# Late loads of a self-product kernel, laid out over 13, 14 and 15 of the 16 DMA engines

## The chip, the cores and the metric

The kernel runs on one core of a Trainium2 chip. The metric is the time of one execution on the device in microseconds (us). The core has five instruction engines (of which this kernel keeps VectorE, GpSimd and SyncE busy; ScalarE helps at the start, TensorE only passes a semaphore on) and 16 DMA engines that carry all transfers between the chip's main memory and its on-chip buffer of 128 partitions.

## The reference

```
dot = jnp.einsum('bi,bj->bij', inputs, inputs)      # inputs: (4096, 256) float32
iu, ju = jnp.triu_indices(256)
return dot[:, iu, ju]                               # (4096, 32896) float32
```

Each of 4096 rows of 256 numbers becomes the 32896 products x[i]*x[j] with i <= j. The input has 4.2 MB, the output 539 MB.

## The kernel before

A partition holds 32 rows of the input. They are worked through in 8 passes (h = 0 to 7) of 4 rows; a pass has two halves of two rows, and each half is cut into three pieces along the 32896 columns. So a pass has six pieces (p = 0 to 5), and there are 48 in all. A piece is computed into one of two places in the on-chip buffer (`places`, 128 partitions x 2 rows x about 10,960 floats) by VectorE (L281) and GpSimd (L382), which multiply runs of the row by one of its numbers, and it is then stored by one transfer that SyncE issues (L410). A store has two packets for each partition, 256 of about 44 KB, so 16 on each of the 16 DMA engines. A place may be filled again only when all packets of its store have landed (the semaphores `free`), so at any time one store is under way and the next is queued behind it.

The input for passes 0, 1 and 2 is loaded by SyncE at the start (L441). The rest comes late, from GpSimd, between its products (`late`, L340 to L361): the unit `ONE` is passes 3 and 4, `EVEN` is pass 5, `TWO` is passes 6 and 7. For a row (a partition) of `ONE` or `TWO` two stretches of 1024 floats are fetched, so two packets of 4 KB; for a row of `EVEN` one packet.

The table `LATE` (L21) says when and how: each line has the pass and piece at whose begin GpSimd issues, the unit, and a list of pairs. The first part of a pair lists the sizes of small loads (`mark`, L325: that many partitions, 64 floats each, into a buffer that nobody reads), the second is the number of partitions that the load proper covers (L354). A load whose count of partitions is 20 is spread over 10 engines with two partitions each, 45 over 15 with three, 3 over three with one, 60 over 15 with four, 128 over all 16 with eight. A load begins on the engine behind the last one of the load before it, all counted around the 16. The marks have only this use: they move the engine on which the next load begins. The table `HAD` (L28) says before which piece GpSimd waits until the loads of a unit, and the marks, have landed (L358 to L361).

Counted through from engine 0, the five lines of the table before give each engine this many 4 KB packets:

| engine | before |
|---|---|
| 4 | 8 |
| 0, 1, 2, 3, 15 | 36 each |
| 5, 9 to 14 | 44 each |
| 6, 7, 8 | 48 each |

Together 640, which is 128 partitions x 5 passes.

Of the kernel before, what the change touches and what calls it, by code (L numbers as in the profile page):

```python
# [18 lines left out]
GAP = 32  # L19
ONE, EVEN, TWO = (3, 4), (5,), (6, 7)  # L20
LATE = [  # L21
    ((1, 3), ONE, [((5,), 20), ((6,), 45)]),
    ((2, 3), ONE, [((2,), 3), ((12,), 60)]),
    ((3, 3), EVEN, [((), 128)]),
    ((4, 3), TWO, [((8, 9), 20), ((6,), 45)]),
    ((5, 3), TWO, [((2,), 3), ((12,), 60)]),
]
HAD = [((2, 5), ONE, 4, 0), ((4, 5), EVEN, 1, 0), ((5, 5), TWO, 4, 9)]  # L28
HELPED = 1
HELP = 16.5  # L30
MARK = 32
# [111 lines left out]
def kernel(  # L143
# [185 lines left out]
    def inputs(of_passes: tuple, rows: slice, lo: int = 0, hi: int = rounds * each) -> tuple:  # L329
        first, last = of_passes[0], of_passes[-1]  # L330
        ends = []
        for ap, at, step in (
            (flat, first * (rounds * each + GAP), (last - first) * (rounds * each + GAP)),
            (x_in, ROUND[first] * rounds * each, (ROUND[last] - ROUND[first]) * rounds * each),
        ):
            dims = [[step, 2], [1, hi - lo]] if step else [[1, hi - lo]]
            ends.append(window(ap[rows, at + lo :], dims))
        return tuple(ends)

    def late(h, p: int):  # L340
        at, rows = 0, {}
        for (begun, piece), of_units, parts in LATE:
            with ExitStack() as when:
                if p == piece:
                    when.enter_context(nc.gpsimd.If(h == begun))
                for steps, count in parts:
# [6 lines left out]
                    if p == piece:  # L353
                        nc.gpsimd.dma_start(*inputs(of_units, slice(row, row + count))).then_inc(far[of_units], 16)  # L354
        for (had, piece), of_units, count, count_of_marks in HAD:
            if p == piece:
# [127 lines left out]
```

## Time and profile before

| | |
|---|---|
| time, median of 3 runs | 1261.2 us (1261.03 to 1261.32) |
| span of the profiled execution | 1259.5 us |
| VectorE busy | 822.7 us, 65% |
| GpSimd busy | 763.5 us, 61% |
| DMA engines | tenths 9 in 39 of 40 slices, 8 in the last |
| bytes | 4.21 MB read, 538.97 MB written, 431 GB/s over the span |

The profiled execution's own time outside the profiler is not listed; its span, from the first to the last instruction, is 1.7 us below the median of the runs. The views used further on are the page with its queues, the waits of the compute engines, GpSimd's timeline around the late loads, and the DMA view of short stretches. In the last one a stretch is cut into 40 slices, and the row GB/s counts a packet's bytes in the slice in which it starts: in a stretch as long as one packet each DMA engine shows up as one spike.

### The profile page before, as it was taken

The numbers are of one execution on the slowest core, as the hardware profiler recorded it, in microseconds if no ns is written. First come the engines' busy times: TensorE is split into PE (matmuls) and PEld (weight loads), VectorE is DVE, ScalarE is ACT, GpSimd is POOL, SyncE is SP. The second block draws the span as 40 slices with busy tenths as digits, with TensorE's granted clock in tenths as the row PEclk, the third lists the DMA queues.
The fourth block names the chain that finished last, engine by engine and source line by source line (L and its number), as shares of the span: only waits on it lengthen the run. The fifth ranks groups of instructions, "written<-read, shape, count | busy, mean of one in ns | idle before, by whom it ended". The sixth has DMA issues, their size and how long they took to land. (4 is left out here: it accounts for less than half of the span.)

```text
span 1259.5 us, 2827 instructions
## 1 busy us (share of the span) xinstructions
DVE 822.7 (65%) x1236; ACT 27.1 (2%) x74; POOL 763.5 (61%) x1149
## 2 busy tenths in 40 slices
DVE  8767657676576665766657675676656766567650
ACT  8000000000000000000000000000000000000000
POOL 5666647665476654766558665576645765467650
DMA  9999999999999999999999999999999999999998
GB/s 396 433 445 423 443 427 433 433 442 427 434 436 432 430 434 435 434 430 441 427 438 433 426 438 427 441 428 438 431 437 428 440 428 437 432 435 432 438 431 380
DMA packets 15911, 543.24 MB, mean 431 GB/s; under 512 B 1440, under 2 KB 1440, under 8 KB 3360
## 3 DMA queue, kind: packets, MB, share of 16 engines
q1 hardware_dynamic: 14704, 540.54, 99.3%
q0 software_dynamic: 1200, 2.64, 0.5%
q14 instruction: 7, 0.06, 0.0%
HBM read 4.21 MB, written 538.97 MB: 431 GB/s over the span
## 5 line engine op out<-in xcount | busy, mean ns | idle before, releaser
L281 DVE TENSOR_TENSOR o<-xv,xp 128x504 f32<-128x504 f32 (+59 forms) x1175 | 791.2, 746 | 398.1 <-DMA out_dram<-o 268.2
L382 POOL TENSOR_TENSOR o<-xv 128x64 f32<-128x64 f32 (+61 forms) x1125 | 751.6, 709 | 450.0 <-DVE o L281 449.8
L309 ACT ACTIVATE o<-x 128x198 f32<-128x198 f32 (+34 forms) x72 | 25.5, 448 | 0.8 <-DMA x<-in_r_inputs_dram 0.8
L260 DVE COPY xp<-x 128x512 f32 x15 | 10.3, 685 | 0.0
L242 DVE TENSOR_TENSOR o<-x,xp 128x470 f32<-128x470 f32 (+18 forms) x19 | 9.7, 585 | 0.0
L242 DVE TENSOR_TENSOR o<-x 128x510 f32<-128x510 f32 (+9 forms) x10 | 5.7, 647 | 2.5 <-DMA x<-in_r_inputs_dram 2.5
L258 DVE COPY xv<-x 128x512 f32 x15 | 6.5, 433 | 0.5
L366 POOL MEMSET xv<- 128x1 f32 x1 | 0.1, 99 | 10.3 <-POOLq L193 10.3
L327 POOL DMA_DIRECT2D marks<-in_r_inputs_dram x9 | 5.7, 637 | 0.4 <-issue 0.3
L354 POOL DMA_DIRECT2D x<-in_r_inputs_dram x9 | 5.5, 615 | 0.0
L444 ACT ACT_TABLE_LOAD x1 | 1.3, 1283 | 1.2 <-ACTq L193 1.2
L442 DVE MEMSET edge<- 128x32 f32 x1 | 0.1, 85 | 1.0 <-SPq L182 1.0
L237 DVE COPY xp<-x 128x512 f32<-128x512 f32 x1 | 0.7, 686 | 0.0
L367 POOL COPY xv<-x 128x512 f32<-128x512 f32 x1 | 0.6, 611 | 0.0
L444 ACT ACTIVATE edge<-edge 128x1 f32<-128x1 f32 x1 | 0.3, 295 | 0.0
L471 POOL MEMSET const-float32-0.0<- 128x1 f32 x1 | 0.1, 99 | 0.2 <-issue 0.2
L471 POOL MEMSET const-bfloat16-1.0<- 128x1 bf16 x1 | 0.1, 103 | 0.0
L471 POOL MEMSET const-uint8-127<- 128x1 uint8 x1 | 0.1, 103 | 0.0
L471 POOL MEMSET const-float32-1.0<- 128x1 f32 x1 | 0.1, 99 | 0.0
## 6 DMA issues: line engine op xcount, KB each, us to landing
out_dram<-o SPq DMA_DIRECT2D x31, 10944.0 KB, 35.2
out_dram<-o SPq DMA_DIRECT2D x16, 11008.0 KB, 32.8
out_dram<-o SPq DMA_DIRECT2D x1, 4352.0 KB, 13.8
out_dram<-o SPq DMA_DIRECT2D x1, 2624.0 KB, 9.4
out_dram<-o SPq DMA_DIRECT2D x1, 1984.0 KB, 7.2
out_dram<-o SPq DMA_DIRECT2D x1, 1280.0 KB, 5.2
x<-in_r_inputs_dram SPq DMA_DIRECT2D x1, 1024.0 KB, 4.9
x<-in_r_inputs_dram POOLq DMA_DIRECT2D x2, 480.0 KB, 29.2
```

The lines of the kernel that those rows point to most:

```text
L237: nc.vector.tensor_copy(xp, x_of(h, 0)).then_inc(v_own, 1)
L242: ins = nc.vector.tensor_tensor(place[:, :, at - lo : at - lo + length], window(x_of(h, 0)[:, j:], [[d, REPEAT], [1, 1], [1, length]]), wi ...
L258: ins = nc.vector.tensor_copy(xv[:, :each], x_of(h, p // PIECES))
L260: nc.vector.tensor_copy(xp, x_of(h, p // PIECES)).then_inc(v_own, 1)
L281: ins = nc.vector.tensor_tensor(place[:, :, at : at + m * length], window(xv[:, j:], [[d, REPEAT], [1, m], [1, length]]), window(xp[:, i:] ...
L309: nc.scalar.activation(places[p][:, r, at - lo : at - lo + length], xa[:, r * d + j : r * d + j + length], AF.Copy, scale=xa[:, r * d + i ...
L327: nc.gpsimd.dma_start(marks[lo:hi, :, :MARK], of).then_inc(marked, 16)
L354: nc.gpsimd.dma_start(*inputs(of_units, slice(row, row + count))).then_inc(far[of_units], 16)
L367: nc.gpsimd.tensor_copy(xv[:, :each], x_of(0, 0)).then_inc(g_own, 1)
L382: ins = nc.gpsimd.tensor_tensor(place[:, :, at : at + m * length], window(xv[:, j:], [[d, REPEAT], [1, m], [1, length]]), window(xv[:, i:] ...
L444: nc.scalar.activation(edge[:, :1], edge[:, 1:2], AF.Copy, scale=edge[:, 2:3])
L471: nc = _bacc.Bacc("TRN2", target_bir_lowering=False, num_devices=1)
```

## The change

Only the two tables are changed. The loads cover other numbers of partitions: 26 and 39 (13 engines with two and three partitions each), 42 and 14 (14 engines with three and one), 60, 75 and 120 (15 engines with four, five and eight), and 8 (eight engines with one). Where a pass loaded 3 and 60 partitions, it now loads 60 or 75 in one transfer; `EVEN`, which was one transfer of 128 partitions, becomes one of 8 and one of 120. The marks have other sizes, and `HAD` has other counts to match: three transfers for `ONE` and `TWO`, two for `EVEN`, eight marks.

```
 LATE = [
-    ((1, 3), ONE, [((5,), 20), ((6,), 45)]),
-    ((2, 3), ONE, [((2,), 3), ((12,), 60)]),
-    ((3, 3), EVEN, [((), 128)]),
-    ((4, 3), TWO, [((8, 9), 20), ((6,), 45)]),
-    ((5, 3), TWO, [((2,), 3), ((12,), 60)]),
+    ((1, 3), ONE, [((5,), 26), ((3,), 42)]),
+    ((2, 3), ONE, [((2,), 60)]),
+    ((3, 3), EVEN, [((), 8), ((9,), 120)]),
+    ((4, 3), TWO, [((8, 9), 39), ((3,), 14)]),
+    ((5, 3), TWO, [((2,), 75)]),
 ]
-HAD = [((2, 5), ONE, 4, 0), ((4, 5), EVEN, 1, 0), ((5, 5), TWO, 4, 9)]
+HAD = [((2, 5), ONE, 3, 0), ((4, 5), EVEN, 2, 0), ((5, 5), TWO, 3, 8)]
```

GpSimd's queue before piece 3 of passes 1 and 2 (each group ends with a branch; `marks` and `x` are the tiles that are loaded, the first number behind them is the count of partitions; - is before, + is after):

```order
 L327 DMA marks<-in_r_inputs_dram 5x2x32
-L354 DMA x<-in_r_inputs_dram 20x2x1024
-L327 DMA marks<-in_r_inputs_dram 6x2x32
-L354 DMA x<-in_r_inputs_dram 45x2x1024
+L354 DMA x<-in_r_inputs_dram 26x2x1024
+L327 DMA marks<-in_r_inputs_dram 3x2x32
+L354 DMA x<-in_r_inputs_dram 42x2x1024
 L343 UNCONDITIONAL_BRANCH
 L345 COMPARE_AND_BRANCH
 L327 DMA marks<-in_r_inputs_dram 2x2x32
-L354 DMA x<-in_r_inputs_dram 3x2x1024
-L327 DMA marks<-in_r_inputs_dram 12x2x32
```

Pass 1 keeps four transfers with other sizes; from pass 2 the load of 3 partitions and the mark of 12 are gone, and the load of 60 follows the mark of 2 directly.

GpSimd's queue before piece 3 of passes 3 and 4, with the same names:

```order
-L354 DMA x<-in_r_inputs_dram 128x1024
+L354 DMA x<-in_r_inputs_dram 8x1024
+L327 DMA marks<-in_r_inputs_dram 9x2x32
+L354 DMA x<-in_r_inputs_dram 120x1024
 L343 UNCONDITIONAL_BRANCH
 L345 COMPARE_AND_BRANCH
 L327 DMA marks<-in_r_inputs_dram 8x2x32
 L327 DMA marks<-in_r_inputs_dram 9x2x32
-L354 DMA x<-in_r_inputs_dram 20x2x1024
-L327 DMA marks<-in_r_inputs_dram 6x2x32
-L354 DMA x<-in_r_inputs_dram 45x2x1024
+L354 DMA x<-in_r_inputs_dram 39x2x1024
```

Pass 3 has three transfers where one stood, pass 4 as many as before with other sizes. In all GpSimd issues 16 transfers where it issued 18. No product moves on any engine.

Counted through from engine 0 in the same way, the changed table gives these counts of 4 KB packets:

| engine | before | after |
|---|---|---|
| 4 | 8 | 1 |
| 3 | 36 | 26 |
| 2 | 36 | 34 |
| 0, 1, 15 | 36 | 44 |
| 5, 9, 10, 11 | 44 | 45 |
| 6, 7, 8 | 48 | 45 |
| 12, 13, 14 | 44 | 44 |

## Rows read from the trace of the kernel before

**Rows 1.** The page: DMA in 40 slices, and the queues (packets, MB, share of 16 engines).
```profile
DMA  9999999999999999999999999999999999999998
...
q1 hardware_dynamic: 14704, 540.54, 99.3%
q0 software_dynamic: 1200, 2.64, 0.5%
```

**Rows 2.** Who waited for whom: us in total, times, longest us.
```profile
POOL o L382 <- DVE o L281: 449.8, 46, 11.1
DVE o L281 <- DMA out_dram<-o: 268.2, 31, 10.2
```

**Rows 3.** The page: stores by issue, KB each, median us from issue to landing.
```profile
out_dram<-o SPq DMA_DIRECT2D x31, 10944.0 KB, 35.2
```

**Rows 4.** Line L354, GpSimd's late loads: from issue to landing.
```profile
DMA to landing us min/median/max: 11.1/19.7/31.8
```

**Rows 5.** GpSimd's timeline, passes 2 and 3: start, us, what, [idle before <- releaser].
```profile
366.58 0.66 POOL L354 DMA_DIRECT2D x<-in_r_inputs_dram  x1
373.96 14.87 POOL L382 TENSOR_TENSOR o<-xv 128x908 f32<-128x908 f32 x12 [6.73 <-DVE o L281]
...
521.40 0.63 POOL L354 DMA_DIRECT2D x<-in_r_inputs_dram  x1
530.65 14.87 POOL L382 TENSOR_TENSOR o<-xv 128x908 f32<-128x908 f32 x12 [8.62 <-DVE o L281]
```

**Rows 6.** Late-load queue in stretches 212:240, 368:398, 525:542, 681:714, 838:867, one row each.
```profile
q0 software_dynamic: 256, 0.54, 4.9%
...
q0 software_dynamic: 256, 0.52, 4.4%
...
q0 software_dynamic: 144, 0.52, 7.5%
...
q0 software_dynamic: 288, 0.54, 4.2%
...
q0 software_dynamic: 256, 0.52, 4.6%
```

**Rows 7.** 1.623 us from 999.062, 1076.708, 1154.354, 1232.0: GB/s in 40 slices each.
```profile
GB/s 0 0 0 0 0 0 2170 1085 0 1085 1085 0 0 0 0 1085 1085 0 0 0 0 0 0 0 0 0 1085 0 0 0 0 1085 1085 0 1085 2170 0 1085 0 1085
...
GB/s 0 0 0 0 0 0 1085 1085 0 1085 1085 0 0 0 1085 1085 1085 0 0 0 0 0 0 0 0 0 1085 0 0 0 0 1085 1085 0 1085 2170 0 1085 0 2170
...
GB/s 0 0 0 0 0 0 1085 1085 0 1085 1085 0 0 0 1085 0 1085 0 0 0 0 0 0 0 0 1085 1085 0 0 0 0 1085 1085 0 1085 2170 0 1085 0 2170
...
GB/s 0 0 0 0 0 0 1085 1085 0 1085 1085 0 0 0 1085 0 1085 0 0 0 0 0 0 0 0 0 1085 0 0 0 0 1085 1085 0 1085 3256 0 1085 0 2170
```

**Rows 8.** The last packets, stretch 1254.599:1256.222: GB/s in 40 slices of 0.0406 us, packets.
```profile
GB/s 1085 0 1085 1085 0 0 0 0 0 1085 1085 0 0 1085 0 0 0 0 1085 1085 0 0 0 0 0 0 0 0 0 0 0 0 0 0 0 0 0 0 1085 0
DMA packets 16, 0.40 MB, mean 244 GB/s; under 512 B 7, under 2 KB 7, under 8 KB 7
```

## The prediction

> **What bounds the kernel now.** I read the page's queues first. The 16 DMA engines are busy in every slice, and the stores' queue alone holds 99.3% of their time [rows 1]. So nothing can be won by computing faster, and the waits say the same from the other side: VectorE stands 268 us waiting for stores to free a place, GpSimd 450 us waiting for VectorE [rows 2]. A store lands 35.2 us after its issue [rows 3], while its 10,944 KB (11.2 MB) at 431 GB/s take 26 us, so about 9 us of the store before it are still ahead of it in the queues. As long as no DMA engine falls more than about 9 us behind another, none runs dry: each of the 16 works through its own list without a gap, and the execution ends when the slowest one has done its list. The question is which one that is, and what the change does to its list.
>
> Two views answer. In stretches as long as one packet each engine is one spike. Four such stretches, each 77.646 us (three stores) behind the last, show fifteen spikes that stay in their slices and one that moves: counting slices from 0, it is the second packet in slice 6, then the one in 14 or 15, then 25, then the third packet in 35 [rows 7]. That is some 10 slices of 0.0406 us, 0.4 us, in 77.6 us: one engine loses about 0.5 us in every 100 us against all others, 6 us over the whole run. Slice 35 of the last stretch is 1233.4; fourteen packets of 1.623 us later it is 1256.15, and in the last stretch that is the start of the very last packet, in slice 38 [rows 8]. So the drifting engine is the one that ends the run. The two behind it start their last packets in slices 18 and 19 (1255.33 and 1255.37), 0.8 us sooner; then come slice 13 (1.0 us sooner), 10 and 9 (1.15), 3, 2 and 0 (1.45 to 1.55); the seven others had started theirs before the stretch, and its seven small packets are their completions, so all sixteen start their last within some 3 us.
>
> Which engine drifts? The price of a load packet is read from pass 3, where the late queue has 144 packets, of which 128 are the 0.52 MB: 7.5% of 16 engines over 17 us are 20.4 us, 0.16 us for each of the 128 [rows 6]. By the count through the table, engine 4 has 8 of them, the others 36 to 48, so it has 28 to 40 x 0.16 = 4.5 to 6.4 us less to do. An engine with that little work and no slowness would end 4 us before the rest. None does; so engine 4 is the one that loses the 6 us. That the count through the table holds is seen in the packets: if a load gives every one of the 16 engines as many packets as the fullest one has, data or a placeholder, and one more to signal, the five lines come to 256, 256, 144, 288 and 256, which are the rows to the packet, 1200 in all [rows 1, 6]. In the first, for instance, marks of 5 and 6 give 32 each, 20 partitions over 10 engines 16 x 5 = 80, 45 over 15 engines 16 x 7 = 112.
>
> Here a page of the Trainium skill states how the engines are chosen: DMA: Bandwidth & Descriptors, section "Why a DMA increments its semaphore by 16 and not by 1", says that GpSimd's loads go to consecutive engines from a round-robin cursor. By that rule the count through the table is right, and the packet counts of this trace agree with it as far as they go (they name no engine).
>
> **The change, part by part.** *The packets that move.* A load packet that takes the place of a small one costs 0.16 less the small one's time. That is about 0.01: in the first stretch 4.9% of 16 x 28 us are 21.9 us, 130 full packets' worth of bytes take 20.7, and some 126 small ones the rest [rows 6]. The new table gives 256, 176, 208, 256 and 208, in all 1104 packets, six fewer on each engine: -0.06 us for all. So:
> - engine 4: 7 load packets fewer, -1.05 - 0.06 = -1.1 us;
> - engine 3: 10 fewer, -1.6; engine 2: 2 fewer, -0.4;
> - engines 0, 1 and 15: 8 more, +1.2 - 0.06 = +1.1;
> - engines 6, 7, 8: 3 fewer, -0.5; engines 5, 9, 10, 11: 1 more, +0.1; engines 12 to 14: -0.06.
>
> All of it lies on the path if the engine is the last one, none if it is not.
>
> *GpSimd's issues.* Pass 3 has two transfers more to issue at 0.6 us each, 1.2 us; there GpSimd then stands idle for 8.6 us until VectorE releases it, so this is hidden; pass 2 (and pass 5, with the same list) has two fewer, and its 6.7 us of idle time only grow [rows 5]. Zero. Without that cover the 1.2 us would go into one piece, and the 9 us of queued store would still hide it.
>
> *When the data is there.* The loads of a line landed 11 to 32 us after the issue [rows 4]; the wait for them stands two pieces later at the soonest, 52 us at 26 us each. In pass 3 three transfers now follow each other, 208 packets where 144 stood, and each of an engine's load packets goes between two stores (7.5% of the time to loads of 0.16 us against stores of 1.6): 13 in place of 9, some 6.5 us longer, used more than a pass later. Zero. Behind the waits for fewer transfers stands GpSimd's last piece of the pass, as before.
>
> *Which engine is last afterwards.* Engine 4 falls by 1.1 and is no longer the last, unless its drift grows. The next two stand at -0.8, and who they are no row says. Of fifteen candidates three rise by 1.1 (0, 1, 15), five fall by 0.4 to 1.6 (2, 3, 6, 7, 8), seven stay. If the three are not among the two latest (12/15 x 11/14 = 0.63 by count alone), then the end moves by -0.8 if those two stay and no one rises past them, by +0.1 if one of the three stood at -1.0, by 0.0 if at -1.15, by -0.4 if at -1.5. I take -0.3, between the two ends, nearer to the engines at -1.15 and -1.5, of which there are five against one at -1.0. If one of the three is among the two latest, the end moves by -0.8 + 1.1 = +0.3.
>
> **The rivals.** *One of engines 0, 1 or 15 becomes the last (slower).* The mechanism above, decided by where that engine ends now: later than 1.1 us ahead of the last, and the run becomes longer. Price up to +0.3 to +0.4: 1261.6. For it: three of the fifteen candidates; against it: only two places are late enough to matter by more than 0.1.
>
> *Engine 15 or 7 is a slow one.* What it would do here: were engine 15 one of the two at -0.8, its 8 packets more would cost up to twice their price, as the slow one's: -0.8 + 2.4 = +1.6, 1262.8. Rows speak against it: only one spike drifts [rows 7], and it is the one with next to no loads. The Trainium skill, DMA: Bandwidth & Descriptors, "Latency and other measured facts", says that engines 7 and 15 are usually slower than the others; by that rule loads would be kept off engine 15, and this trace does not bear it out.
>
> *The loads don't land where the count says.* If the first load begins on another engine than in the run before, the drifting engine gets 44 or 45 packets in place of 8: 36 x 0.15 = +5.4, 1266.6. Against it: the five lines move the starting engine by 148 in all, both before and after, so even a start that is carried on from one execution to the next would be carried alike, and the small spread of the runs, 0.3 us, shows no such jumps.
>
> *It does nothing:* the last engine stays where it was because the drift takes what the loads give back, 1261.2.
>
> **How the numbers follow.** The span is 1259.5, the median 1261.2; I take the 1.7 us around the span as unchanged. Forecast: 1261.2 - 0.3 = 1260.9, with 0.58. One of 0, 1, 15 last, 1261.6: 0.29. No change, 1261.2: 0.06. Engine 15 slow, 1262.8: 0.04. Another start, 1266.6: 0.03. The range reaches from the lower end of the forecast with the runs' spread, 1261.2 - 0.8 - 0.3 = 1260.1, to the upper end of the first rival with it and a little of the loads' contention, 1262.0. About 0.2%, 2.5 us, is what a measurement of this kernel can tell from no change. Only another start (0.03) and the far end of a slow engine 15 (0.01) lie above; nothing computed lies below, 0.02 is left for a drift of engine 4 that loads make worse than I saw. So 0.02, 0.94 and 0.04.
>
> **What would show it.** In the profile of the changed kernel the late queue has 1104 packets with 256, 176, 208, 256 and 208 by pass; if not, the spreading is another than I counted. In the last stretch the latest spike is no longer alone by 0.8 us: the last engines end closer together, within 0.5 us. If the drifting spike is still the last by as much, the drift, and not the loads, decides. If a steady spike is the last, later than in the run before, one of engines 0, 1 and 15 has become the bound. GpSimd's idle time before its products in pass 3 should fall from 8.6 to about 7.4 us with no other trace of it. The prediction is wrong if the time moves by more than 1 us either way: then the engines' lists are not what ends the run, or the stores themselves are slowed where loads pass.

## The result

| | before | after |
|---|---|---|
| time, median | 1261.12 us (1260.73 to 1261.53, 17 runs) | 1263.43 us (1263.13 to 1263.83, 17 runs) |
| ratio | | 1.0019, 95% interval 1.0012 to 1.0026 |
| span of the profiled execution | 1259.5 us | 1262.0 us |

The changed kernel is slower by 2.3 us, some 0.2%, where 1260.9 us was forecast. The profiled execution itself took 1263.83 us.

The signs that the prediction named for the packets and for GpSimd came out as it said; that the last engines would end closer together did not. The queues of the page (packets, MB, share of 16 engines), which answer [rows 1]:

```profile
DMA  9999999999999999999999999999999999999997
...
q1 hardware_dynamic: 14704, 540.54, 99.1%
q0 software_dynamic: 1104, 2.63, 0.5%
```

1104 packets of late loads, as counted. By pass, the stretches 212:241, 368:390, 525:549, 681:712 and 838:865, which answer [rows 6]:

```profile
q0 software_dynamic: 256, 0.56, 4.9%
...
q0 software_dynamic: 176, 0.49, 5.6%
...
q0 software_dynamic: 208, 0.53, 5.5%
...
q0 software_dynamic: 256, 0.44, 3.7%
...
q0 software_dynamic: 208, 0.62, 5.6%
```

256, 176, 208, 256 and 208 were foretold. GpSimd's timeline in pass 3 (start, us, what, [idle before <- releaser]), beside [rows 5]:

```profile
520.99 0.61 POOL L354 DMA_DIRECT2D x<-in_r_inputs_dram  x1
521.59 0.60 POOL L327 DMA_DIRECT2D marks<-in_r_inputs_dram  x1
522.19 0.58 POOL L354 DMA_DIRECT2D x<-in_r_inputs_dram  x1
530.29 14.88 POOL L382 TENSOR_TENSOR o<-xv 128x908 f32<-128x908 f32 x12 [7.51 <-DVE o L281]
```

The two added transfers took 1.2 us out of idle time, 8.62 became 7.51, and the products began no later than before. So none of these shows the loss. It shows at the end. The stretch 1254:1260 in 40 slices of 0.15 us (GB/s by the slice in which a packet starts, 294 is one packet), first of the kernel before:

```profile
GB/s 0 294 587 1174 881 0 587 294 294 294 0 0 0 0 294 0 0 0 0 0 0 0 0 0 0 0 0 0 0 0 0 0 0 0 0 0 0 0 0 55
```

and of the changed kernel:

```profile
GB/s 294 0 1174 587 587 294 0 587 0 294 0 294 0 0 294 0 0 0 0 0 294 0 0 0 0 0 0 0 0 0 0 294 0 0 0 0 0 0 0 0
```

Before, the last packet starts in slice 14 (slices from 0; the 55 is an instruction packet). Now it starts in slice 31, 2.5 us later. Slices 20 and 31 are one packet's time apart, so they are the same engine, and behind slice 14 only that engine starts another store packet. Which one it is shows in stretches of one packet's length, 1.623 us from 1079.646, 1157.292 and 1234.938, which answer [rows 7]:

```profile
GB/s 2170 0 1085 1085 0 2170 1085 0 0 0 0 1085 0 0 0 0 1085 0 2170 0 0 1085 0 1085 0 0 0 0 0 0 1085 0 0 0 0 0 0 1085 0 1085
...
GB/s 2170 0 1085 1085 0 1085 1085 0 0 0 0 1085 0 0 0 1085 1085 0 2170 0 0 1085 0 1085 0 0 0 0 0 0 1085 0 0 0 0 0 0 1085 0 1085
...
GB/s 2170 0 1085 1085 0 1085 1085 0 0 0 0 1085 0 0 0 0 1085 0 2170 0 0 1085 0 1085 1085 0 0 0 0 0 1085 0 0 0 0 0 0 1085 0 1085
```

One spike moves: the second packet in slice 5, then slice 15, then 24. That is again some 10 slices of 0.0406 us in 77.6 us, no faster than before. From slice 24 of the last stretch, 1235.92, fourteen packets of 1.623 us lead to 1258.65, which is slice 31 above. So the drifting engine is still the last, its drift is the same, and it ends 2.5 us later than before, though the count gave it seven load packets less. So it should have got more of them than in the kernel before: at 0.15 us each, some 17.

### The profile page after: what moved, and what is told of

It is laid out like the page before. It is cut to its first block, busy times and chain, and to the rows that moved or that the text cites. A ratio compares the mean times of both kernels' runs of the same rounds, so it can differ in the third digit from the quotient of the medians.

```text
span 1262.0 us, 2825 instructions
## 1 busy us (share of the span) xinstructions
DVE 822.8 (65%) x1236; ACT 27.1 (2%) x74; POOL 762.3 (60%) x1147
## 3 DMA queue, kind: packets, MB, share of 16 engines
q0 software_dynamic: 1104, 2.63, 0.5%
## 5 line engine op out<-in xcount | busy, mean ns | idle before, releaser
L354 POOL DMA_DIRECT2D x<-in_r_inputs_dram x8 | 4.9, 617 | 0.0
```

## The experiments

Two kinds of loads can be told apart in this kernel. `ONE`, `TWO` and the marks fetch two stretches (runs of addresses without a gap) for each partition, `EVEN` (pass 5) one. In the kernel before, `EVEN` is a single transfer over all 16 engines, so it tells nothing of where a load of its kind begins. In the changed kernel it is two transfers, with a mark between them. Theory A: a load with one stretch for each partition begins on engine 0 whatever stood before, has ceil(partitions / 16) of them on each engine, and does not move the start of the next load. Then the load of 8 lies on engines 0 to 7 and the load of 120 on 0 to 14, engine 4 among them both times, and the mark of 9, which should have closed the circle with them, alone turns the starts of passes 4 and 5 by nine engines. Engine 4 gets 1 + 8 packets in pass 3, 6 + 2 in pass 4 and 10 in pass 5: 27. Theory B: the loads lie where the table's count says, and the new sizes, or stores slowed beside them, cost the time. Engines are numbered by the count; the trace names none. All times below are medians against runs of the kernel before on the same chip, and lines of `HAD` that only follow the number of transfers are left out of the edits.

**e1: pass 5 loaded in one transfer again, without the mark of 9, all else as changed.**

```
-    ((3, 3), EVEN, [((), 8), ((9,), 120)]),
+    ((3, 3), EVEN, [((), 128)]),
```

> The changed kernel with pass 5's load put back to one transfer of 128 partitions, everything else as changed. Theory A (a load with a single stretch for each partition, as pass 5's are, begins on engine 0 whatever stood before and does not move the next start): the marks and loads of passes 4 and 5 then lie where the table means them to, the drifting engine 4 has 8 load packets as in the kernel before, the loss is gone: 1261.1 us, between 1260.7 and 1261.6. Theory B (the loads lie where the count says, and the other new sizes, 26, 39, 42, 14 and 75, or the stores slowed beside them, cost the time): the loss stays, 1263 us or more.

Measured: 1260.60 us against 1260.73, ratio 0.9998 (0.9989 to 1.0007). The whole loss is gone, with the loads of 26, 42, 60, 39, 14 and 75 still in place. (The time lies 0.1 us below the range of theory A, which was reckoned from 1261.2 for the kernel before.)

**e3: the kernel before with pass 5's load alone changed.**

```
-    ((3, 3), EVEN, [((), 128)]),
+    ((3, 3), EVEN, [((), 8), ((9,), 120)]),
```

> The kernel before with pass 5's load alone changed (8 partitions, mark of 9, 120 partitions). Theory A: the mark of 9 turns the starts of passes 4 and 5 by nine engines, so engine 4 gets 9 packets in pass 3, 10 in pass 4 and 8 in pass 5, 27 in place of 8: 19 x 0.15 = 2.8 less the small packets, 1263.4 us, between 1262.9 and 1264.2. Theory B: the count says that engine 4 has 1 packet; no loss, 1260.3 to 1261.3 us.

Measured: 1263.55 against 1260.73, ratio 1.0022 (1.0013 to 1.0031). This one line carries the whole loss. Its last packets, in the same stretch 1254:1260:

```profile
GB/s 587 294 294 587 294 294 294 587 294 294 0 294 0 0 294 0 0 0 294 0 0 0 0 0 0 0 0 0 0 294 0 0 0 0 0 0 0 0 0 0
```

Slices 18 and 29 are one engine, alone behind all others as in the changed kernel. e3 does not tell the two loads from the mark between them; e4 does.

**e4: the changed kernel without the mark of 9.** This tells how pass 5's loads move the start, for here the theories stand the other way round: if the loads of 8 and 120 moved it, leaving out the mark would bring the loads of passes 4 and 5 onto engine 4.

```
-    ((3, 3), EVEN, [((), 8), ((9,), 120)]),
+    ((3, 3), EVEN, [((), 8), ((), 120)]),
```

> The changed kernel without the mark of 9 between the loads of 8 and 120 partitions. Theory A: these two loads don't move the start, so without the mark passes 4 and 5 lie as the table means them; engine 4 has 1 + 8 packets from pass 3 and no other: 9, 1261.2 us, between 1260.7 and 1261.7. Theory B, where every load moves the start by its engines: without the mark pass 4 begins on engine 11 and engine 4 gets 1 + 8 + 8 + 10 = 27 packets: 1263.4 us or more. The two theories stand the other way round than in the changed kernel itself.

Measured: 1260.75 against 1260.73, ratio 1.0001 (0.9992 to 1.0010), within theory A's range. Same stretch:

```profile
GB/s 294 0 1468 1174 0 294 294 587 294 0 0 294 0 0 0 0 0 0 0 0 0 0 0 0 0 0 0 0 0 0 0 0 0 0 0 0 55 0 0 0
```

The last packet is back in slice 11, with the others close before it. The trace's packet records, followed engine by engine through pass 3 of this run, agree: eight engines have a packet of the load of 8 and eight packets of the load of 120, seven have the latter only, one has neither. Had the load of 120 begun behind the one of 8, it would have reached all eight engines without the first and seven of the eight with it.

**e2: pass 5 in two stretches.** The count through the table, carried out: pass 5's rows are fetched as two stretches of 504 floats for each partition, and the 2 x 8 floats left over in a small transfer, with a mark of 2.

```
-    ((3, 3), EVEN, [((), 8), ((9,), 120)]),
+    ((3, 3), EVEN, [((), 8), ((2,), 120)]),
...
+            if halves:
+                dims = [[each, halves], [1, hi - lo]]
...
-                        nc.gpsimd.dma_start(*inputs(of_units, slice(row, row + count))).then_inc(far[of_units], 16)
+                        cuts = [(0, each - 8, 2), (each - 8, each, 2)][:: -1 if row else 1] if of_units == EVEN else [()]
+                        for cut in cuts:
+                            to_from = inputs(of_units, slice(row, row + count), *cut)
+                            nc.gpsimd.dma_start(*to_from).then_inc(far[of_units], 16)
```

> The changed kernel with pass 5's rows fetched as two stretches of 504 floats for each partition and a small transfer for the eight floats behind each, with a mark of 2 in place of the one of 9, so that by the count through the table engine 4 gets 2 packets of 2 KB in all, and the small ones. Theory A, if loads of two stretches do move the start: engine 4 has about 1.1 us less to do than in the kernel before, and the next engines end the run: 1260.2 to 1261.7 us, 1260.9 by the prediction's own sum. If loads of two stretches of pass 5 too begin on engine 0: 1263 us or more. Theory B: 1263 us or more, since the other sizes are those of the changed kernel.

Measured: 1261.08 against 1260.73, ratio 1.0003 (0.9994 to 1.0012). The same 8 and 120 partitions, in two stretches, cost nothing that can be told. So it is the kind of load and not its count of partitions. Followed engine by engine, the load of 120 leaves out one engine, and that is the drifting one, as the count had it. Same stretch:

```profile
GB/s 294 294 1468 587 587 294 294 587 0 294 0 294 294 0 0 0 0 0 0 0 0 0 0 0 0 0 0 0 0 0 0 0 0 0 0 0 0 55 0 0
```

Slices 11 and 12, and 9 before them: the last engines now end together, within the 0.5 us that the prediction had named for the plan. The time gains nothing that can be told, since the next engines stand right behind.

**e5 and e6: the price of a packet on engine 4.** If engine 4 is slow in itself, any shift of the starts that loads it must show. e5 makes the kernel before's first mark 6 in place of 5 (all starts one further, engine 5 left out, 36 packets on engine 4); e6 adds a mark of 14 (all starts two back, engine 2 left out, 48 packets on engine 4).

```
-    ((1, 3), ONE, [((5,), 20), ((6,), 45)]),
+    ((1, 3), ONE, [((6,), 20), ((6,), 45)]),        # e5
+    ((1, 3), ONE, [((5, 14), 20), ((6,), 45)]),     # e6
```

> The kernel before with its first mark of 6 in place of 5, so that every start of a two-stretch load lies one engine further. Theory A with the slow engine fixed: the engine left out is now engine 5, and the drifting engine 4 has 36 load packets in place of 8: 28 x 0.15 = 4.2, 1265.0 us, between 1264.3 and 1265.8; the last packet of the run starts some 5 us behind the next. Rival C (the drift goes with the engine that is left out by the loads, through its many placeholders): the drift moves along to engine 5 and the time stays within 0.5 us of before.

> The kernel before with another mark of 14 behind its first one of 5, so that every later start lies two engines back (14 further). Theory A with the slow engine fixed: engine 2 is left out, and the drifting engine 4 has 48 load packets in place of 8: 40 x 0.15 = 6.0, 1266.8 us, between 1266.0 and 1267.7. Rival C: within 0.5 us of before.

Measured: e5 1264.82 against 1260.78, ratio 1.0031 (1.0019 to 1.0044), +4.04 for 28 packets; e6 1266.49, ratio 1.0045 (1.0028 to 1.0062), +5.71 for 40. Both 0.14 us a packet. The slow engine stays where it is, and rival C (the drift goes with the engine that the loads leave out) falls. The last packets of e6, stretch 1255.5:1261.5, 0.15 us a slice:

```profile
GB/s 2642 0 294 0 0 294 0 294 0 0 0 0 0 0 0 0 294 0 0 0 0 0 0 0 0 0 0 294 0 0 0 0 0 0 0 0 0 0 294 0
```

Spikes 5, 16, 27 and 38 are one engine, a packet's time apart; behind slice 7 it is alone, for 4.7 us.

**e7: marks of one stretch.** Theory A on loads of another kind: the kernel before with its marks as one stretch of 64 floats in place of two of 32.

```
-        of = window(x_in[lo:hi], [[2 * MARK, 2], [1, MARK]])
-        nc.gpsimd.dma_start(marks[lo:hi, :, :MARK], of).then_inc(marked, 16)
+        of = window(x_in[lo:hi], [[1, 2 * MARK]])
+        nc.gpsimd.dma_start(marks[lo:hi, 0, :], of).then_inc(marked, 16)
```

> The kernel before with its marks as one stretch of 64 floats for each partition in place of two of 32; number, place and bytes of the marks are as before. Theory A: no mark moves a start any more, so the loads of passes 1, 2, 4 and 5 begin at 0, 10, 9, 12, 11, 5, 4 and 7, and engine 4 gets 4 + 6, 8, 8, 4 and 2 + 8 packets, 40 in place of 8: 32 x 0.15 = 4.8, 1265.5 us, between 1264.7 and 1266.3. Theory B (what the number of partitions sets, whatever the stretches): within 0.5 us of before.

Measured: 1265.39 against 1260.78, ratio 1.0036 (1.0023 to 1.0048), +4.61 for 32 packets, 0.144 us each. Not a byte, a partition or a load was changed; only the shape of transfers that nobody reads. So marks of one stretch move no start; that a load of this kind also begins on engine 0 is shown by the followed packets, in e4 and below.

**e8: is the drift SyncE's?** The stores, with their waits, are issued from ScalarE.

```
-                store = nc.sync.dma_start(to, place[:, :, lo:hi])
+                store = nc.scalar.dma_start(to, place[:, :, lo:hi])
```

> The kernel before with the stores issued from ScalarE in place of SyncE; since ScalarE first computes until about 14 us, the first stores begin some 9 us later and the time is longer for that alone, about 1270 us. Looked for is the drift: if it belongs to SyncE's issuing, it moves to another engine, one that has 36 to 48 load packets, and the last packet starts 4 to 6 us behind the next; if it belongs to engine 4 itself, the last engines end as close together as in the kernel before, within about 1 us.

Measured: 1280.85, ratio 1.0159 (1.0138 to 1.0179). That ScalarE would first compute until 14 us was wrong; it works through both early pieces, and the first store is issued at 25.06:

```profile
3.70 21.63 ACT L309 ACTIVATE o<-x 128x256 f32<-128x256 f32 x61 [0.89 <-DMA x<-in_r_inputs_dram]
...
25.06 0.42 ACTq L410 DMA_DIRECT2D out_dram<-o  x1
```

In the kernel before the first store is issued at 4.80, 20.3 us sooner, about as much as the time has grown, 20.1:

```profile
4.80 9.22 SPq L410 DMA_DIRECT2D out_dram<-o  x4
```

The end of e8, stretch 1271.5:1277.5:

```profile
GB/s 881 294 0 294 587 294 294 1761 294 0 587 587 0 0 294 587 294 294 1761 294 0 587 587 0 0 0 587 294 0 0 0 0 0 0 0 0 0 0 0 0
```

The last three packets start in slices 26 and 27, so the engines end together and no engine with 36 to 48 load packets has taken over the drift. It does not go with SyncE's issuing. What else slows engine 4 stays open.

**The drifting engine's own packets.** The packet records show that engine directly, for each packet of an engine starts 3 or 4 ns before the end of its last one. In a stretch without loads (590 to 670 us, in e8 610 to 690) one engine's store packets take 1.626 to 1.628 us on average in each of the ten runs, those of the other fifteen 1.618. This engine has these 4 KB load packets from the five lines of the table:

| kernel | its load packets | in all |
|---|---|---|
| before, e1, e8 | 0, 0, 8, 0, 0 | 8 |
| changed | 0, 0, 9, 8, 10 | 27 |
| e3 | 0, 0, 9, 10, 8 | 27 |
| e4 | 0, 0, 9, 0, 0 | 9 |
| e5 | 6, 8, 8, 6, 8 | 36 |
| e7 | 10, 8, 8, 4, 10 | 40 |

That is theory A's count in every line, and theory B's 1 for the changed kernel is not among them. In its pass 3 the mark of 9 touches four of the eight engines that the load of 8 reaches and five of the seven others that the load of 120 reaches, just as engines 4 to 12 stand to 0 to 7 and 0 to 14.

## Why the prediction was wrong, point by point

- *What bounds the kernel* was right: each DMA engine's list, the drifting engine's last. The prediction's own sign against this, a time that moves by more than 1 us, came up and was misread there: the lists still end the run, only other packets stand on them. e5, e6 and e7 bear it out with 4.04, 5.71 and 4.61 us for nothing but packets moved onto that engine.
- *Engine 4 drifts* was right, argued from what little it had to do; e5 and e6 show it, since the time follows that engine's count and not the engine that is left out. So the rivals with engine 15, or 0 or 1, as the last one did not come about; no run shows that a packet costs a slow engine twice, as the sum for engine 15 had it (0.144 us on engine 4).
- *The price of a packet* was right: 0.15 us in the sum, 0.144, 0.144 and 0.143 measured.
- *"That the count through the table holds is seen in the packets"* is the step that failed. The number of packets was right to the packet in both kernels, but it only says how many engines a load uses, not on which it begins, and both kinds of loads give the same number. So the rows could not bear the sentence that was put on them. That a load begins behind the last engine of the load before it, as the part ahead of the prediction says, is true here of loads with two stretches only, and the row of engine 4 in its table, 8 and 1, should have been 8 and 27. The term "engine 4: 7 load packets fewer, -1.1" should have been 19 more: 19 x 0.15 less 0.06 for the small packets, +2.8. Measured were +2.3 in the time and +2.5 at the last packet; e3, with the same 27 packets, has +2.8. The 0.5 us that the changed kernel stays below the sum are not explained.
- The Trainium skill's page DMA: Bandwidth & Descriptors, section "Why a DMA increments its semaphore by 16 and not by 1", on which the prediction drew, also states an exception: some direct copies from GpSimd are spread over all 16 engines with ceil(partitions / 16) partitions on each, and copies over 16 engines are not placed by the cursor. The prediction used the rule and passed over the exception. The page does not say which copies these are; e2, e4 and e7 show that here it is those with one stretch for each partition: followed engine by engine, the load of 120 lies on 15 engines with eight partitions each.
- *The rival "the loads don't land where the count says"* was the right one, with a chance of 0.03. It was sought in a start that differs between executions, and dismissed for that: 148 moves before and after. That sum itself took the loads of 8 and 120 for moves, 23 in all, though the one load of their kind in the kernel before, over 16 engines, could not show any. Its price, 1266.6, was that of a rotation of all passes; only the loads issued in passes 3, 4 and 5 lie elsewhere than counted.
- *GpSimd's issues* and *when the data is there* cost nothing, as said.
- *What the plan would have brought* had it been carried out is e2: +0.35 us against the -0.3 of the forecast and the +0.3 of the first rival, with an interval of about 1.1 us either way. The runs don't tell these apart. e1 and e4, with 8 and 9 packets on engine 4, are as fast: once that engine ends with the others, taking more from it buys nothing that these runs can tell.

None of the eight kernels is measurably faster than the kernel before.

## What to carry to other kernels

When all DMA engines are full to the end, time follows the one engine that ends last, so ask of each small transfer on which engine it lies, not only on how many. A count that two placements share proves neither: look for a case in the trace in which they differ, and if the kernel before has none, give that rival a real chance. Changing a transfer's shape (one stretch for each partition or two) can move all later ones, even if the transfer carries nothing.

## What the runs showed of the hardware

- GpSimd's loads with one stretch for each partition begin on engine 0 and leave the next start alone; those with two stretches begin where the last one of their kind ended (27 packets on the drifting engine where the count had 1; without the mark of 9, 9). Marks of one stretch in place of two alone cost 4.61 us (e7).
- One engine of the 16 is slower at stores by about 0.5 us in 100 us, before and after [rows 7]: its packets take 1.626 to 1.628 us on average, the others' 1.618. By the count it is engine 4 in all these runs, whichever engine the loads leave out (e5, e6) and whichever engine's queue the stores are issued from (e8).
- A 4 KB load packet between two stores costs its engine 0.143 to 0.144 us more than the small one in its place, over 28, 32 and 40 packets (e5, e7, e6).
